# A gather-and-scatter graph layer: two tiles in 48 fetched row by row on two queues, three kinds of copies moved to VectorE, and first halves of 104 columns

## The chip, the cores and the metric

The kernel runs on one core of one Trainium2 chip. A core has five engines that run their own instruction streams and wait for each other through semaphores: TensorE (PE, with its weight loads as PEld), VectorE (DVE), ScalarE (ACT), GpSimd (POOL) and SyncE (SP). ACT, POOL and SP can start DMAs. The metric is the device time of one execution in microseconds (us); the median of three runs before the change is 2020.3 us (2017.76 to 2020.92).

## The reference

One graph layer with pre-normalisation: layer norm and ReLU over 12,500 nodes of 256 features, then, for 212,500 edges sorted by destination, the sum over a node's edges of its source's row times the weight of the edge's type (8 types), a self product, a bias, and the input added. Every node has one self-loop, the last of its edges, and about 16 others.

```python
h = jnp.maximum(_layernorm(x, axis=-1), 0.0)
hx = jnp.einsum('ni,rio->rno', h, weight)
agg = segment_sum(hx[edge_type, src], dst, num_segments=12500)
out = x + agg * 0.5**0.5 + h_bias + (h @ loop_weight) * 0.5**0.5
```

## The kernel before

**Units, tiles, windows.** The kernel sums rows of h by destination and type first and multiplies by the weights afterwards. Edges are cut into 802 units. The first 128 units have 256 edges each; the next ones 267 edges, of which each node's last edge (its self-loop) is taken out and the 256 others are kept, packed to the front of the unit (`compacted`); the last unit has the 41 edges that are left. A unit is one or two tiles of 128 kept edges: first half and second half (1603 tiles, the last unit has one). A unit's destinations lie in a window of WIN = 22 nodes that starts at `base`, the unit's first destination held between two bounds that lines 1082 to 1088 compute; the last of these holds both bounds between 0 and N - WIN.

For each tile a one-hot matrix of 128 edges by 22 x 8 columns (node in the window and type) is made on DVE (line 785), from a column number for each edge that `columns` computes (lines 481 to 585). `REACH` says from which node of the window each half's columns begin and how many nodes they span; an edge whose column lies outside is masked (line 558 for units of 267, lines 503 and 507 for the first block) and its column becomes 0. PE multiplies the gathered rows by the one-hot (line 818, fp32) into a PSUM bank, DVE adds the bank to a ring of sums `acc` (line 832), and when a group of 128 nodes is complete, 18 matmuls (line 1009) and two additions (1021, 1022) give its output.

**Gathers.** Rows come from x, for the first tiles, later from h32, the normalised table in HBM. POOL gathers a tile with one indirect DMA (line 755), 58 tiles ahead, into one of 60 slots. Of every 48 tiles one is not gathered by POOL: SP reads 16 byte offsets at a time from the tile `single` (line 762) and starts one DMA of 1 KB for each row (line 767), four list entries for each tile step (`fetch`), from 8 tile steps after the gather would have been issued. SP's queue also carries the loads of x, h, edges and weights and the stores of the output.

**Self-loops.** `find_types` finds the type of each node's self-loop and `begin` writes the node's own row into the ring through a PSUM tile `pt` (line 881). Three kinds of copies there run on ACT: `self_t` from `pt` (line 864, 98), a diagonal (line 934, 88) and the types (line 945, 22).

**The verdict.** Each unit counts the edges that its masks and its self-loops cover. `verdict` (lines 613 to 631) adds the counts, compares them with E and sets `flag`; every engine reads the flag, and at line 1243 the program branches: where the flag is set, `general_path` (lines 120 to 216) computes all of the output once more, with one node tile or 128 edges a round.

```python
# 622   def differs(): nc.vector.tensor_scalar(flag, pt[0:1, 0:1], float(E), None, op0=ALU.not_equal)
# 1087  nc.vector.tensor_scalar(
# 1088      whole, f, 0.0, float(max(0, N - WIN)), op0=ALU.max, op1=ALU.min)
# 210   for body, total in ((nodes, N), (edges, E)):
# 212       with tc.For_i(0, total // P * P, P) as i:
# 213           body(i, P)
# 1243  with tc.If(state["general"]):
# 1244      general_path(tc, x, src, dst, etype, bias, out, h32, w, wl, ident)
```

`nodes` (lines 146 to 171) loads 128 rows of h32 and x, transposes h, multiplies it by the self weight and by the eight type weights, one PSUM tile after another, and stores 1 MB of products into `hx` and the self part into `gacc`. `edges` (lines 173 to 208) loads source, destination and type of 128 edges and the destinations as a row (lines 179, 183), makes two columns of row numbers on DVE, gathers 128 rows of `hx` (line 199), adds those of equal destination with one matmul (line 203), copies the result out of PSUM and adds it to `gacc` with an indirect DMA (line 206). All pools of general_path have one buffer. At the end `gacc` is copied to the output (line 216).

Of the kernel before, what the change touches and what calls it, by code (L numbers as in the profile page):

```python
# [13 lines left out]
AF = mybir.ActivationFunctionType  # L14
ALU = mybir.AluOpType
# [3 lines left out]
SYNC_DEP = mybir.DependencyInfo(mybir.DependencyClass.Sync, mybir.DependencyReason.DATA)  # L19
DVE = mybir.EngineType.DVE  # L20
SP = mybir.EngineType.SP

P = 128
EPS = 1e-5
# [3 lines left out]
XG = 4  # L28
# [4 lines left out]


WIN = 22
REACH = ((0, 22), (4, 18))

GROUP = 128

# [5 lines left out]
AHEAD = 58  # L45

SINGLE = 48
FETCH = 4
SOURCES = 16
HOLD = 8  # L50


# [2 lines left out]
PAIR = 2  # L55
# [164 lines left out]
def kernel(  # L220
# [11 lines left out]
    nc = tc.nc  # L232
    N, D = x.shape
    E = src.shape[0]
    R = weight.shape[0]
# [5 lines left out]
    NT = plan.NT  # L241
# [33 lines left out]

    def place_of(t):
        u, i = divmod(t, PAIR)
        return u // P, i, u % P


    with ExitStack() as main:
# [29 lines left out]
        msg, oh, offsets, kind = {}, {}, {}, {}  # L311
        firsts, stops, loops, marked, typed, gidx, col = {}, {}, {}, {}, {}, {}, {}
        added, zeroed = {}, {}
        single, fetches = {}, []
        state = {"h32": None}


# [39 lines left out]
        def kept_sources(b, got):  # L357

            def keep():
                single[b] = idx.tile([P, P], I32, name="single")  # L360
                nc.vector.tensor_single_scalar(
                    single[b], got["sf"][:, P:U], float(D * 4), op=ALU.mult)

            return [keep]

# [115 lines left out]
        def columns(b, got):  # L481
# [22 lines left out]
                        got["there"][:, h], got["col"][:, h], float(o), None, op0=ALU.is_ge)  # L504

            def plain_to():
                nc.vector.scalar_tensor_tensor(
                    got["there"][:, :U], got["col"][:, :U], float(WIN), got["there"][:, :U],
                    op0=ALU.is_lt, op1=ALU.mult)

            def plain_typed():
                nc.vector.scalar_tensor_tensor(
# [226 lines left out]
        def gather(t):  # L739
            if t % PAIR == 0:  # L740
                both = msgs.tile([P, PAIR, D], F32, name="msg")
                for i in range(PAIR):
                    msg[t + i] = both[:, i, :]
            if t % QUAD:
                kind[t] = kind[t - 1]
            else:
                kind[t] = "h" if state["h32"] is not None and t >= state["h32"] + LATE else "x"
            table = {"h": h32, "x": x}[kind[t]]
            b, i, u = place_of(t)
            if b and i and kind[t] == "h" and t % SINGLE == SINGLE - 1 and t + AHEAD < NT:  # L750
                for r in range(0, P, SOURCES):
                    fetches.append((done["tile"] + HOLD, lambda r=r: load_sources(t, r)))
                return
            at = i * P + u
            nc.gpsimd.indirect_dma_start(  # L755
                out=msg[t], out_offset=None, in_=table[:, :],
                in_offset=bass.IndirectOffsetOnAxis(ap=gidx[b][:, at : at + 1], axis=0))

        def load_sources(t, r0):

            b, _, u = place_of(t)
            _, vals = nc.values_load_multi_w_load_instructions(  # L762
                single[b][u : u + 1, r0 : r0 + SOURCES], engines=[SP],
                min_val=0, max_val=(N - 1) * D * 4,
                skip_runtime_bounds_check_because="clamped to the table where they are computed")
            for i, v in reversed(list(enumerate(vals))):
                fetches.insert(0, (0, lambda i=i, v=v: nc.sync.dma_start(  # L767
                    msg[t][r0 + i : r0 + i + 1, :].bitcast(U8),
                    h32_bytes[:, bass.ds(v, D * 4)])))

        def fetch(n):
            for _ in range(n):
                if fetches and fetches[0][0] <= done["tile"]:
                    fetches.pop(0)[1]()

        def onehots(t):

            n = min(QUAD, NT - t)
            o = ohs.tile([P, QUAD // PAIR, PAIR, C], F32, tag="oh", name="oh")
            b, _, u = place_of(t)  # L780
            k = 0
            for v, i in ((n // PAIR, PAIR), (1, n % PAIR)):
                if v and i:
                    of = col[b].rearrange("p (i u) -> p u i", i=PAIR)[:, u + k : u + k + v, :i]
                    j = nc.vector.tensor_tensor(  # L785
                        o[:, k : k + v, :i, :],
                        iota_f.unsqueeze(1).unsqueeze(1).to_broadcast([P, v, i, C]),
                        of.unsqueeze(3).to_broadcast([P, v, i, C]), op=ALU.is_equal)
                    k += v
            for i in range(n):  # L790
                oh[t + i] = o[:, i // PAIR, i % PAIR, :]
                made[t + i] = j.ins.name

        def load_offsets(u0):
# [8 lines left out]
        def edge_sums(t):  # L803
            m, o = msg.pop(t), oh.pop(t)
            if t % PAIR == 0:
                bank = banks[t // PAIR % BANKS]
                sums["ps"] = bank[:, : KC * R * WIN].rearrange("p (c k) -> p c k", c=KC)
            ps = sums["ps"]
            i = t % PAIR
            from_, width = (a * R for a in REACH[i])  # L810
            end = t == NT - 1 or i == PAIR - 1
            free = added.get(t // PAIR - BANKS)
            if i == 0 and free is not None and latest["pe"] is not None:
                tc.add_manual_dep(latest["pe"], free.name, SYNC_DEP, reason="bank is free")
            if i == 0 and latest["pe"] is not None:
                tc.add_manual_dep(latest["pe"], made[t], SYNC_DEP, reason="one-hots are made")
            for c in range(KC):
                j = nc.tensor.matmul(  # L818
                    ps[:, c, from_ : from_ + width], m[:, c * P : (c + 1) * P], o[:, :width],
                    start=(i == 0 and c == 0), stop=(end and c == KC - 1))  # L820
            latest["pe"] = j.ins
            return ps
# [28 lines left out]
        def turn_nodes(g, pool, written=None):  # L851

            n = plan.ends[g] - plan.starts[g]
            pst = pt[:, : KC * P].rearrange("p (c d) -> p c d", c=KC)

            def turn():
                rows_ = got["h", g // XG][:, g % XG, :]
                for c in range(KC):
                    nc.tensor.transpose(  # L859
                        pst[:, c, :n], rows_[:n, c * P : (c + 1) * P], ident[:n, :n])  # L860

            def keep():
                got["self", g] = pool.tile([P, KC, GROUP], F32, name="self_t")
                i = nc.scalar.activation(got["self", g][:, :, :n], pst[:, :, :n], AF.Copy)  # L864
                if written:
                    tc.add_manual_dep(
                        i.ins, written[0].name, SYNC_DEP, reason="one reader at a time")

            return turn, keep, pst

        def begin(g):

            n = plan.ends[g] - plan.starts[g]
            q, k = divmod(g, XG)
            written = []
            turn, keep, pst = turn_nodes(g, selves, written)
            s0 = g % SLOTS * GROUP

            def own(r):
                of = typed[q][:, k * GROUP : k * GROUP + n].unsqueeze(1).to_broadcast([P, KC, n])  # L880
                i = nc.vector.scalar_tensor_tensor(  # L881
                    acc[:, :, r, s0 : s0 + n], of, float(r + 1), pst[:, :, :n],
                    op0=ALU.is_equal, op1=ALU.mult)
                if r == R - 1:
                    zeroed[g, "slot"] = i.ins
                    written.append(i.ins)
# [20 lines left out]
        def find_types(q):  # L907
# [11 lines left out]
            def kinds_of():  # L919
# [45 lines left out]
        def group_ahead(g):  # L965
# [11 lines left out]
            if q < plan.typed:  # L977
                def turned_nodes():
                    turn, keep, _ = turn_nodes(g, early)
                    shared(turn, [(1, keep)])  # L980

                work.append((0.4, turned_nodes))
            if k == XG - 2:
# [286 lines left out]
```

## Time and profile before

| what | value |
|---|---|
| median of 3 runs | 2020.3 us |
| the profiled execution, its time | 2023.05 us |
| its span, first to last instruction | 2021.3 us |
| mean granted clock of PE | 0.957 |
| DMA, mean over the span | 139 GB/s |
| matmuls with one-hots, line 818: 128x176 / 128x144 | 645.8 / 562.2 us busy |
| matmuls with weights, line 1009, on sums | 883.0 us busy |
| ACT copies of line 864 / 934 / 945 | 37.5 / 28.1 / 13.1 us busy |
| SP's row DMAs, line 767 | 3456 of 1 KB, 228 ns each at the queue |
| SP's register loads, line 762 | 216, median 1261 ns |

A profile row has a line of the program, an engine and an operation with a count, the busy time and the mean of one; after the bar stands how long the engine sat idle just before, and what ended that. "issue" is time in which an engine waited for nothing that the profile shows. The timeline gives start, duration, engine, line and count; the chain of waits goes back from the last instruction to what released it at each step. SPq, ACTq, POOLq and so on are the sequencers in front of the engines.

### The profile page before, as it was taken

Reading aid. Unit: us, or ns where it says so; the run is one execution under the profiler, and the core shown is the slowest. Engines: PE = TensorE matmul, PEld = TensorE weight load, DVE = VectorE, ACT = ScalarE, POOL = GpSimd, SP = SyncE. Lnnn points to the kernel's source line nnn. Section 1 sums busy time; section 2 is a strip of 40 time slices with the busy share of each in tenths; the row PEclk is TensorE's granted clock in tenths of the full one; section 3 lists DMA queues with packets and bytes.
Section 4 is the critical chain, followed back from the end, with each engine's and each line's share of the span. In section 5 each row is a group of like instructions: output and inputs, shape, how many; then the busy total and the mean of one; then the engine's idle time right before and its main releaser. Section 6 shows DMA issues by size and latency. Waiting matters only on the chain.

```text
span 2021.3 us, 36386 instructions
## 1 busy us (share of the span) xinstructions
PE 1796.2 (89%) x10411; PEld 1610.0 (80%) x10411; DVE 1317.4 (65%) x3281; ACT 218.4 (11%) x470; POOL 1500.7 (74%) x1602
## 2 busy tenths in 40 slices
PE   2468999997999898999899999998998898998998
PEld 2357999997888888988788788787787787787886
DVE  7869566687656578656577655577665568665642
ACT  7854110000000000000000000000000000000000
POOL 7766777777777777777777777777777777777773
PEclk8569999998999999999999999999999999999999
DMA  8973443444444444444444444444444444444442
GB/s 296 380 222 97 146 138 106 128 138 127 129 139 118 139 137 117 130 118 139 130 126 139 128 124 135 132 122 140 129 118 138 125 123 129 118 138 123 118 120 73
DMA packets 152577, 281.63 MB, mean 139 GB/s; under 512 B 31149, under 2 KB 101940, under 8 KB 152372
## 3 DMA queue, kind: packets, MB, share of 16 engines
q0 software_dynamic: 75648, 206.67, 35.1%
q1 hardware_dynamic: 76724, 72.61, 11.4%
q8 instruction: 82, 1.34, 0.3%
q14 instruction: 123, 1.01, 0.2%
HBM read 253.55 MB, written 25.60 MB: 138 GB/s over the span
## 4 chain that ended last, share of the span: by engine, by line
PE 38%; DMA 20%; SPq 17%; issue 12%; POOL 7%; DVE 5%; ACT 2%; DVEq 0%; POOLq 0%; ACTq 0%
PE ps L818 20%; PE po L1009 17%; DMA msg<-h,gidx 13%; SPq L767 13%; POOL msg L755 7%; SPq L762 4%; DMA hr<-h 2%; DMA h<-xt 1%; DVE e_stats L701 1%; DVE acc L832 1%; ACT xt L713 1%; DMA xr<-in_x_dram 1%; DMA w<-in_L_gnn_weight_dram 1%; DMA msg<-h 1%; DVE oh L785 1%
## 5 line engine op out<-in xcount | busy, mean ns | idle before, releaser
L755 POOL DMA_INDIRECT msg<-h,gidx x1480 | 1407.7, 951 | 464.2 <-issue 371.1
L818 PE MATMUL ps<-oh,msg 128*128 128x176 f32 (+1 forms) x6412 | 1169.6, 312 | 201.5 <-DMA msg<-h,gidx 78.5
L818 PEld LDWEIGHTS ps<-oh,msg 128*128 128x128 f32 x6412 | 1037.8, 196 | 355.3 <-DMA msg<-h,gidx 159.1
L1009 PE MATMUL po<-w,acc 128*128 128x256 f32 x3136 | 883.0, 383 | 1.8 <-DVE acc L832 1.8
L832 DVE TENSOR_TENSOR acc<-acc,ps 128x352 f32 x802 | 415.1, 518 | 503.4 <-PE ps L818 499.1
L1009 PEld LDWEIGHTS po<-w,acc 128*128 128x128 f32 x3136 | 537.6, 192 | 25.3 <-DVE acc L832 2.6
L785 DVE TENSOR_TENSOR oh<-fixed,cols 128x704 f32<-128x704 f32 x402 | 353.0, 879 | 0.0
L881 DVE SCALAR_TENSOR_TENSOR acc<-types,pt 128x256 f32<-128x256 bf16 (+1 forms) x688 | 249.0, 411 | 77.5 <-PE pt L859 71.5
L864 ACT ACTIVATE self_t<-pt 128x256 f32<-128x256 f32 x98 | 37.5, 383 | 1456.4 <-DVE acc L881 1352.5
L755 POOL DMA_INDIRECT msg<-in_x_dram,gidx x96 | 91.0, 948 | 31.1 <-issue 24.4
L1009 PE MATMUL po<-wl,self_t 128*128 128x256 f32 x392 | 105.2, 391 | 4.9 <-ACT self_t L864 2.5
L1009 PEld LDWEIGHTS po<-wl,self_t 128*128 128x128 f32 x392 | 69.1, 196 | 11.4 <-ACT self_t L864 2.9
L1021 DVE TENSOR_TENSOR xr<-xr,po 128x256 f32<-128x256 f32 x98 | 40.5, 413 | 17.5 <-PE po L1009 15.7
L713 ACT ACTIVATE xt<-xt,n_shift,n_rstd 128x256 f32<-128x256 f32 x98 | 50.9, 588 | 8.6 <-DVE n_shift L710 8.6
L713 ACT ACTIVATE msg<-msg,e_shift,e_rstd 128x256 f32<-128x256 f32 x96 | 49.6, 589 | 12.8 <-DVE e_shift L710 12.8
L1022 DVE TENSOR_TENSOR xr<-xr,po 128x256 f32<-128x256 f32 x98 | 41.2, 420 | 3.4
L934 ACT ACTIVATE diagonal<-ident,kinds 128x128 bf16<-128x128 f32 x88 | 28.1, 390 | 135.0 <-DVE kinds L931 130.1
L859 PE MATMUL pt<-ident,hr 128*128 128x128 f32 x196 | 37.9, 275 | 0.0
L370 DVE TENSOR_SCALAR moves<-fixed 128x267 int32<-128x267 int32 x84 | 36.0, 428 | 1.1
L701 DVE BATCH_NORM_STATS2 n_stats<-xt 128x6 f32<-128x256 f32 x98 | 34.4, 412 | 2.5 <-DMA xt<-in_x_dram 1.7
L371 DVE COPY_PREDICATED fixed<-moves,fixed 128x266 int32<-128x266 int32 (+6 forms) x84 | 33.7, 401 | 2.9
L701 DVE BATCH_NORM_STATS2 e_stats<-msg 128x6 f32<-128x256 f32 x96 | 33.5, 411 | 0.0
(201 smaller groups left out, 319.7 us busy)
## 6 DMA issues: line engine op xcount, KB each, us to landing
msg<-h SPq DMA_DIRECT2D x3456, 1.0 KB
msg<-h,gidx POOLq DMA_INDIRECT x1480
xt<-in_x_dram SPq DMA_DIRECT2D x24, 512.0 KB
h<-xt SPq DMA_DIRECT2D x24, 512.0 KB
xr<-in_x_dram SPq DMA_DIRECT2D x24, 512.0 KB
hr<-h SPq DMA_DIRECT2D x24, 512.0 KB
out_dram<-xr SPq DMA_DIRECT2D x24, 512.0 KB
w<-in_L_gnn_weight_dram SPq DMA_DIRECT2D x2, 1024.0 KB
```

Of the source, the lines that this page charges most:

```text
L701: nc.vector.bn_stats(stats[:n, j, :], rows_[j])
L713: nc.scalar.activation(rows_[j], rows_[j], AF.Relu, bias=shift[:n, j : j + 1], scale=rstd[:n, j : j + 1])
L755: nc.gpsimd.indirect_dma_start(out=msg[t], out_offset=None, in_=table[:, :], in_offset=bass.IndirectOffsetOnAxis(ap=gidx[b][:, at : at + 1 ...
L762: _, vals = nc.values_load_multi_w_load_instructions(single[b][u : u + 1, r0 : r0 + SOURCES], engines=[SP], min_val=0, max_val=(N - 1) * D ...
L767: fetches.insert(0, (0, lambda i=i, v=v: nc.sync.dma_start(msg[t][r0 + i : r0 + i + 1, :].bitcast(U8), h32_bytes[:, bass.ds(v, D * 4)])))
L785: j = nc.vector.tensor_tensor(o[:, k : k + v, :i, :], iota_f.unsqueeze(1).unsqueeze(1).to_broadcast([P, v, i, C]), of.unsqueeze(3).to_broa ...
L818: j = nc.tensor.matmul(ps[:, c, from_ : from_ + width], m[:, c * P : (c + 1) * P], o[:, :width], start=(i == 0 and c == 0), stop=(end and ...
L832: i = nc.vector.tensor_tensor(a, a, ps, op=ALU.add)
L881: i = nc.vector.scalar_tensor_tensor(acc[:, :, r, s0 : s0 + n], of, float(r + 1), pst[:, :, :n], op0=ALU.is_equal, op1=ALU.mult)
L1009: i = nc.tensor.matmul(got["out", g][:n], lhs, rhs, start=(r == R and c == 0), stop=(r == R - 1 and c == KC - 1))
L1021: nc.vector.tensor_add(rows_[:n, k, :], rows_[:n, k, :], outs[g % 2][:n, 1, :])
L1022: nc.vector.tensor_add(rows_[:n, k, :], rows_[:n, k, :], got["out", g][:n])
```

## The change

SP fetches tiles 47 of 48 as before and ACT's queue, in the same manner, tiles 23 of 48; both read 32 offsets at a time. The two halves change places: the tile with the kept edges 128 to 255 comes first, over all 22 nodes of the window, and the tile with the first 128 comes second, over nodes 0 to 12, so 13 x 8 = 104 columns. A last unit with one tile keeps its edges in the first half. The copies of lines 864, 934 and 945 go from ACT to DVE (the four diagonals of a group of four as one operation). Line numbers behind line 21 grow by one to three. general_path, the verdict and lines 1082 to 1088 stay as they are.

```diff
-REACH = ((0, 22), (4, 18))
+REACH = ((0, 13), (0, 22))
-SOURCES = 16
+SOURCES = 32
     def place_of(t):
         u, i = divmod(t, PAIR)
-        return u // P, i, u % P
+        half = 0 if PAIR * u + 1 == NT else PAIR - 1 - i
+        return u // P, half, u % P
-        single, fetches = {}, []
+        single, fetches = {}, {SP: [], ACT: []}
...
-                    single[b], got["sf"][:, P:U], float(D * 4), op=ALU.mult)
+                    single[b], got["sf"][:, :P], float(D * 4), op=ALU.mult)
...
             def plain_to():
-                nc.vector.scalar_tensor_tensor(
-                    got["there"][:, :U], got["col"][:, :U], float(WIN), got["there"][:, :U],
-                    op0=ALU.is_lt, op1=ALU.mult)
+                for h, o, n in halves:
+                    nc.vector.scalar_tensor_tensor(
+                        got["there"][:, h], got["col"][:, h], float(o + n), got["there"][:, h],
+                        op0=ALU.is_lt, op1=ALU.mult)
...
-            if b and i and kind[t] == "h" and t % SINGLE == SINGLE - 1 and t + AHEAD < NT:
-                for r in range(0, P, SOURCES):
-                    fetches.append((done["tile"] + HOLD, lambda r=r: load_sources(t, r)))
-                return
+            if b and t % PAIR and kind[t] == "h" and t + AHEAD < NT:
+                engine = {SINGLE - 1: SP, SINGLE // 2 - 1: ACT}.get(t % SINGLE)
+                if engine is not None:
+                    for r in range(0, P, SOURCES):
+                        fetches[engine].append(
+                            (done["tile"] + HOLD, lambda r=r: load_sources(t, r, engine)))
+                    return
...
-                single[b][u : u + 1, r0 : r0 + SOURCES], engines=[SP],
+                single[b][u : u + 1, r0 : r0 + SOURCES], engines=[engine],
...
+            queue = {SP: nc.sync, ACT: nc.scalar}[engine]
             for i, v in reversed(list(enumerate(vals))):
-                fetches.insert(0, (0, lambda i=i, v=v: nc.sync.dma_start(
+                fetches[engine].insert(0, (0, lambda i=i, v=v: queue.dma_start(
...
-            from_, width = (a * R for a in REACH[i])
+            width = R * (REACH[0][1] if i else WIN)
...
-                    ps[:, c, from_ : from_ + width], m[:, c * P : (c + 1) * P], o[:, :width],
+                    ps[:, c, :width], m[:, c * P : (c + 1) * P], o[:, :width],
...
-                i = nc.scalar.activation(got["self", g][:, :, :n], pst[:, :, :n], AF.Copy)
-                if written:
-                    tc.add_manual_dep(
-                        i.ins, written[0].name, SYNC_DEP, reason="one reader at a time")
+                nc.vector.tensor_copy(got["self", g][:, :, :n], pst[:, :, :n])
...
-                for g in range(XG):
-                    nc.scalar.activation(
-                        marked[q][:, g * GROUP : (g + 1) * GROUP], ident, AF.Copy,
-                        scale=kinds[:, g : g + 1])
+                nc.vector.tensor_tensor(
+                    marked[q].rearrange("p (g k) -> p g k", g=XG),
+                    ident.unsqueeze(1).to_broadcast([P, XG, GROUP]),
+                    kinds.unsqueeze(2).to_broadcast([P, XG, GROUP]), op=ALU.mult)
...
-                nc.scalar.activation(typed[q], pt, AF.Copy)
+                nc.vector.tensor_copy(typed[q], pt)
-            shared(spread, [(1, types_of)], lambda: q in marked, wait=2)
+            shared(spread, [(2, types_of)], lambda: q in marked, wait=2)
```

More of the change, by code (lines that the diff above doesn't have):

```diff
@@ L21 @@
 SP = mybir.EngineType.SP
+ACT = mybir.EngineType.Activation
 P = 128
@@ L757, in gather, with load_sources @@
                 in_offset=bass.IndirectOffsetOnAxis(ap=gidx[b][:, at : at + 1], axis=0))
-        def load_sources(t, r0):
+        def load_sources(t, r0, engine):
             b, _, u = place_of(t)
             _, vals = nc.values_load_multi_w_load_instructions(
-                single[b][u : u + 1, r0 : r0 + SOURCES], engines=[SP],
+                single[b][u : u + 1, r0 : r0 + SOURCES], engines=[engine],
                 min_val=0, max_val=(N - 1) * D * 4,
                 skip_runtime_bounds_check_because="clamped to the table where they are computed")
+            queue = {SP: nc.sync, ACT: nc.scalar}[engine]
             for i, v in reversed(list(enumerate(vals))):
-                fetches.insert(0, (0, lambda i=i, v=v: nc.sync.dma_start(
+                fetches[engine].insert(0, (0, lambda i=i, v=v: queue.dma_start(
                     msg[t][r0 + i : r0 + i + 1, :].bitcast(U8),
@@ L771, in fetch @@
         def fetch(n):
-            for _ in range(n):
-                if fetches and fetches[0][0] <= done["tile"]:
-                    fetches.pop(0)[1]()
+            for list_ in fetches.values():
+                for _ in range(n):
+                    if list_ and list_[0][0] <= done["tile"]:
+                        list_.pop(0)[1]()
         def onehots(t):
@@ L790, in onehots @@
             for i in range(n):
-                oh[t + i] = o[:, i // PAIR, i % PAIR, :]
+                oh[t + i] = o[:, i // PAIR, place_of(t + i)[1], :]
                 made[t + i] = j.ins.name
@@ L849, in clear, with turn_nodes @@
             zeroed[g, "slot"] = i.ins
-        def turn_nodes(g, pool, written=None):
+        def turn_nodes(g, pool):
             n = plan.ends[g] - plan.starts[g]
@@ L874, in begin @@
             q, k = divmod(g, XG)
-            written = []
-            turn, keep, pst = turn_nodes(g, selves, written)
+            turn, keep, pst = turn_nodes(g, selves)
             s0 = g % SLOTS * GROUP
@@ L885, in own @@
                     zeroed[g, "slot"] = i.ins
-                    written.append(i.ins)
             def write():
@@ L979, in turned_nodes @@
                     turn, keep, _ = turn_nodes(g, early)
-                    shared(turn, [(1, keep)])
+                    shared(turn, [(2, keep)])
                 work.append((0.4, turned_nodes))
```

## The prediction

> **What bounds the kernel now.** I read the page first (busy shares, slices, groups), then the timeline of POOL and SP, then the chain of waits, then the events of the two lines where the program branches and ends.
>
> ```profile
> PE 1796.2 (89%) x10411; PEld 1610.0 (80%) x10411; DVE 1317.4 (65%) x3281; ACT 218.4 (11%) x470; POOL 1500.7 (74%) x1602
> ...
> POOL 7766777777777777777777777777777777777773
> ...
> L755 POOL DMA_INDIRECT msg<-h,gidx x1480 | 1407.7, 951 | 464.2 <-issue 371.1
> ```
>
> PE has the largest share, but POOL's row is the flat one: 7 in nearly every slice, and most of the idle time before its gathers is issue, a wait for nobody. The timeline of POOL, and that of SP's queue, say what a 7 is:
>
> ```profile
> 1003.51 0.94 POOL L755 DMA_INDIRECT msg<-h,gidx  x1 [0.30 <-issue]
> 1004.76 0.95 POOL L755 DMA_INDIRECT msg<-h,gidx  x1 [0.31 <-issue]
> ...
> 1008.52 0.95 POOL L755 DMA_INDIRECT msg<-h,gidx  x1 [0.30 <-issue]
> ```
> ```profile
> 863.00 51.86 SPq L767 DMA_DIRECT2D msg<-h  x128
> ```
>
> One gather every 1.252 us ((1008.52 - 1003.51) / 4), back to back: POOL is full. 1576 gathers at 1.252 are 1973 us, from 4.75 to 1996.6 us; PE waits for what they bring (78.5 us at matmuls and 159.1 at weight loads, in the view of waits) and then has some 25 us of its own. SP fetches 27 tiles in POOL's place, 51.9 us each.
>
> The chain of waits gives the durations of DMAs (start, us, what), from issue to landing:
>
> ```profile
> 0.82 2.06 DMA nat_s<-in_src_dram
> ...
> 48.44 5.29 DMA h<-xt
> ...
> 405.00 6.01 DMA nat_t<-in_edge_type_dram
> ...
> 1778.62 5.86 DMA msg<-h,gidx
> ...
> 1979.16 2.73 DMA msg<-h,gidx
> ```
>
> And the lines of the branch on the verdict (L1243) and of the end of the program (L1266), the sequencers' own events (count, min/median/max ns, first and last start):
>
> ```profile
> L1243 SPq EVENT_SEMAPHORE  x8: 17/17/17, 2018.2 to 2019.6; - x8
> ...
> L1243 POOLq COMPARE_BRANCH  x1: 45/45/45, 1989.1 to 1989.1; - x1
> L1243 POOLq INC_SWDGE_SEM  x1: 2016/2016/2016, 1993.3 to 1993.3; - x1
> ```
> ```profile
> L1266 SPq EVENT_SEMAPHORE  x14: 17/28/28, 2019.7 to 2021.3; - x14
> ```
>
> Each engine compares once and goes to the end; no line of general_path is in the trace. Whether that stays so decides this case.
>
> **The change, part by part: the windows.** The first half of a unit (its first 128 kept edges) may now lie in columns 0 to 12 of its window alone. For a unit whose window starts at its first node that is ample. But L1088 holds every window's start at or below N - WIN = 12500 - 22 = 12478. The last unit has 212500 - 32768 - 673 x 267 = 41 edges, and in the drawn inputs they begin at node 12498, as every node has a self-loop and some 16 more. Its offset is 12498 - 12478 = 20. Its 39 edges that are not self-loops belong to columns 20 and 21, and all lie in the first half. Before, the first half reached 22 columns, and they counted. Now L558 admits column numbers up to 13 x 8 = 104, and theirs begin at 20 x 8 + 1 = 161: their mask is 0. So counts adds up to 212461, not E = 212500, differs at L623 gives 1, and the branch at L1243 goes into general_path, which computes everything again. (Of the unit before, the offset is small enough; I find no other miss.) The integers are far below 2^24, and in the run of before the same comparison came out equal.
>
> **The cost of general_path.** The trace has no row of it, so each step is bounded by its nearest rows. All its pools have one buffer, and each round of its loops ends with all engines waiting for each other and for every DMA: nothing overlaps from round to round, so a round is the sum of its chain.
>
> A round of edges (1660, and one of 20 edges):
> - SP issues four loads. The kernel's first three started at 0.82, 1.28 and 1.75, 0.46 apart, and the first landed after 2.06; the third, the types, lands at 0.1 + 2 x 0.46 + 2.06 = 3.1 us. Upper end 7.0, with the 6.01 of nat_t. I take 3.1: nothing else moves then.
> - DVE casts the types (0.14, as L394) and makes the row number (0.16, as L600): 0.3. The other nine DVE operations lie before it or under the gather.
> - The gather: 2.73 to 5.86; 2.8, for an idle chip.
> - PE, one product of 256 columns: weights 0.19 and the pair of passes 0.59, 0.8; at half clock 1.6 (the window 50 to 100 us shows 0.50 granted).
> - DVE's copy out of PSUM: 0.47 with its gap (L351, 0.42).
> - The scatter that adds: no row. At least a gather, 2.73; at most one under load, 5.86; it also reads what it adds to. I take 4.1, between.
> - The end of the round: SP's last events run from 2019.6 to 2021.3, 1.7 us for the waits and two meetings of all engines; POOL's semaphore instruction has one row of 2.0 that may itself be a wait. 1.7 to 4.0, and 2.9 taken.
>
> Sum 14.5 us (11.9 to about 20 with several upper ends at once): 1661 x 14.5 = 24,085 us.
>
> A round of nodes (98): load 2.6 (issue 0.49, then as nat_s), transposes 0.4, copy 0.4, own product 0.9, eight times two products (0.86), a copy (0.42) and gaps (0.1), as the one PSUM tile makes them alternate, 11.0; the store of 1 MB, 0.5 and twice the 5.29 of the 512 KB store, 10.6; end 2.9. 28.8 us, so 2820 us in all. 22 to 40 us a round (store half as long; PE at half clock): 2150 to 3900.
>
> At last 12.8 MB go from gacc to the output: between 380 GB/s (the page's best slice) and its mean of 139, 34 to 92 us; 65 taken, and 10 for the set-up.
>
> **The other parts**, which change the first 2 ms. SP's queue keeps its 27 tiles; ACT takes 27 more from POOL: 27 x 1.252 = 33.8 us less on the path that sets the end. What hides the rest: a row costs SP (51.86 - 8 x 1.3) / 128 = 0.324 us, a tile 41.5 plus four register loads of 32 (1.26, L762's row for 16, to 2.52), 47 to 52 us, within the 46 x 1.252 = 57.6 between two such tiles. ACT has no DMA row in the trace; SP's is the nearest, and above 57.6 / 128 - 0.06 = 0.39 us a row ACT would become the bound. In ACT's queue nothing stands behind these rows in that stage, since its 98 copies (383 ns), 88 diagonals (390) and 22 types (597) move to DVE: about 98 x 0.42 + 22 x 0.66 + 22 x 0.66 = 70 us on an engine busy 1317 of 2021, hidden while DVE waits for PE (499 us before L832); without that cover 70 us more. The first halves' matmuls shrink from 144 to 104 columns: the chain has 0.60 us for a tile of 176 and 0.49 for one of 144, so 0.35 for 104, or 0.49 if the weight loads bind: 0 to 112 us of PE time, worth nothing while PE waits for gathers. The mask of the first block is made in two operations instead of one, and the halves change places: nothing that anyone waits for.
>
> **Sum**, against the profiled execution's 2021.3 us span: 2021.3 - 33.8 = 1987.5; + 2820 + 24,085 + 65 + 10 = 28,968. Some 1.75 us lie outside the span (2023.05), and the median, 2020.3, is 2.75 below that; next to 27 ms neither counts. I forecast 29,000 us.
>
> **Rivals.**
> - *The verdict holds and general_path is not entered* (the other side). Place: the compare at L1243; it decides if the last unit's window does not start at 12478. Then the time is 1987.5, and the 27 ms vanish. For it: the trace shows the branch not taken. Against: the sum above is integer arithmetic on the inputs. 0.03.
> - *Not entered, and ACT's queue binds*: at 0.45 us a row a tile takes 65 us, and 27 of them 1760 from about 340 us on, some 2110. 0.01: it needs the first miss too.
> - *Each round fetches its instructions anew.* The page's instruction queues show 82 and 123 packets for a program that runs straight on; no row shows a jump back. If each round waits for one or two DMAs at 2.06 us, 1759 rounds add 3600 to 7200, and the time is about 34,000. 0.15. The Trainium skill (Runtime: NRT & Kernel Launch, section Instruction fetch mechanics) speaks for it: a taken branch to code outside the two pages that an engine holds must wait for a DMA of that page. No run here shows it yet.
> - *Rounds overlap*, so that the loads and the gather of the next run under the scatter: some 8 us a round (5.5 for gather and scatter, 2.9 for the end), 18,000 in all. Against: one buffer for each tile and the wait at each round's end. 0.08.
>
> **How the numbers follow.** The forecast, general_path at about 14.5 us a round, has 0.73. Low end 23,000: 1987 + 2150 + 19,765 (11.9 a round) are 23,900, with a little room. High end 38,000: 20 us a round and 40 for nodes give 39,000 with nearly all upper ends at once; it also holds the refetching rival. What is left out is the two rivals at 2 ms, the overlap and a little at the top, under 0.2. A difference of 0.2% is about what a measurement can tell. Faster takes the first rival, 0.03; same 0.01, in case gains and ACT's cost cancel; slower 0.96.
>
> **What would show it.** Right: rows for L149 to L216 (shifted by the new lines), 1660 scatters on POOL, a PE row near 0 after slice 3, and POOL's last gather of msg near 1963 us. Wrong: a span near 1990 without such rows; or a round far from 14.5 us, and then the step whose duration differs. The fetch on ACT is right if PE does not wait for msg rows longer than before and the first stage ends 30 to 36 us sooner.

## The result, and the profile after

The changed kernel takes 27,488.57 us (median of 4 runs, 27,459.43 to 27,540.62), the kernel before 2019.53 us in runs beside it: 13.61 times as long (95% interval 13.591 to 13.639). The profiled execution took 27,540.62 us, with a span of 27,538.9 us. 29,000 us were predicted, 23,000 to 38,000.

The page of the changed kernel (rows of engines; tenths of busy time in 40 slices; costliest groups with busy time, mean ns and the idle time before):

```profile
PE 5303.2 (19%) x17457; PEld 3390.3 (12%) x17457; DVE 6275.1 (23%) x24434; ACT 140.2 (1%) x262; POOL 5748.4 (21%) x4900
...
PE   7766555300000000000000000000000000000000
...
POOL 7652000111111111111111111111111111111111
PEclk8887555555555555555555555555555555555555
...
L200 POOL DMA_INDIRECT g_m<-hx,g_of x1661 | 1643.2, 989 | 14405.7 <-DVE g_of L197 11648.4
L207 POOL DMA_INDIRECT gacc<-g_ss,g_to x1661 | 2630.1, 1583 | 6414.7 <-DVE g_ss L206 6414.7
...
L761 POOL DMA_INDIRECT msg<-h,gidx x1453 | 1381.4, 951 | 822.2 <-issue 370.1
...
L826 PE MATMUL ps<-oh,msg 128*128 128x176 f32 (+1 forms) x6412 | 1107.2, 305 | 632.5 <-DMA msg<-h 552.9
```

From line 21 on, lines stand one to eight further down than before: 818 is now 826, 832 is 840, 1243 is 1246. Lines 200 and 207 are general_path's gather and scatter: 1661 of each, one a round. A slice is 688 us. The first stage fills three and a half, the rounds of nodes the next four, and in the last 32 no engine is busy for more than two tenths. The last two rows tell of something else, in the first stage: POOL sat idle 822 us before its gathers (464 before the change), and PE 553 us for rows of `msg`.

The events of the branch (line 1243 before, 1246 now: count, min/median/max ns, first and last start):

```profile
L1246 POOLq COMPARE_BRANCH  x2: 48/48/49, 2321.4 to 27492.4; - x2
...
L1246 SPq COMPARE_BRANCH  x2: 37/45/53, 2401.1 to 27496.3; - x2
```

Each engine branches twice now, once into general_path and once at its end. SP, the last, enters at 2401 us and is back at 27,496: the first stage ends at 2402 instead of 2021, and everything behind it takes 25,137 us, of which the copy of `gacc` to the output is the last 42. Nodes run from 2402 to 5147, 28.0 us for each of 98 rounds; edges from 5147 to 27,497, 13.45 us for each of 1661.

The timeline of one edge round (start, duration, engine, line):

```profile
15000.37 0.15 DVE L181 CAST g_sf<-g_s 128x1 f32<-128x1 int32 x1 [7.33 <-DMA g_s<-in_src_dram]
...
15002.00 0.99 POOL L200 DMA_INDIRECT g_m<-hx,g_of  x1 [7.09 <-DVE g_of L197]
...
15004.94 1.19 PE L204 MATMUL g_ps<-g_m,g_same 128*128 128x256 f32 x2 [12.36 <-DMA g_m<-hx,g_of]
15006.17 0.42 DVE L206 COPY g_ss<-g_ps 128x256 f32<-128x256 f32 x1 [1.78 <-PE g_ps L204]
15006.87 1.58 POOL L207 DMA_INDIRECT gacc<-g_ss,g_to  x1 [3.89 <-DVE g_ss L206]
15011.72 0.33 SPq L179 DMA_DIRECT2D g_s<-in_src_dram  x1
```

and a piece of the chain of waits in the last rounds:

```profile
27481.02 3.86 DMA gacc<-g_ss,g_to
```

Nothing overlaps from round to round. From the gather's issue to PE are 2.9 us, PE takes 1.2 at half clock, and from its end to the scatter's issue are 0.7. By the events of the scatter's semaphore, it lands 3.8 us after its issue in the median (3.65 in the round shown, at 15,010.5), and the next round's first load starts 1.2 us behind the landing (0.87 to 1.24 in 1660 rounds).

The first stage, in windows of 400 us (busy us and instructions of PE, PEld, DVE, ACT, POOL; granted clock; DMA share; GB/s). After, and then before:

```profile
800.00:1200.00 400.00, 302.70 (x1802) 281.07 (x1800) 224.35 (x516) 0.00 (x0) 246.38 (x260) 0.87 0.37 107
```
```profile
800.00:1200.00 400.00, 367.03 (x2161) 332.52 (x2160) 256.94 (x586) 17.45 (x46) 302.69 (x320) 0.97 0.44 129
```

POOL issues 260 DMAs where it issued 320: it is no longer full. The view of waits (us in all, times, longest) before:

```profile
PE ps L818 <- DMA msg<-h: 45.5, 11, 10.4
```

and after:

```profile
PE ps L826 <- DMA msg<-h: 552.9, 34, 26.0
```
```profile
SPq L774 <- DMA msg<-h: 425.2, 783, 10.0
```

PE waited 34 times, up to 26 us, for tiles that were fetched row by row (11 times, 45.5 us in all, before), and SP's queue 783 times for the landing of a row before it issued one. The timelines of SP's and of ACT's queue (consecutive DMAs of one line are one entry):

```profile
1299.87 58.23 SPq L774 DMA_DIRECT2D msg<-h  x116
1358.20 0.41 SPq L1030 DMA_DIRECT2D out_dram<-xr  x1
1358.67 0.50 SPq L962 DMA_DIRECT2D hr<-h  x1
1364.32 13.78 SPq L774 DMA_DIRECT2D msg<-h  x32
```
```profile
1300.05 79.98 ACTq L774 DMA_DIRECT2D msg<-h  x151
```

Before, SP issued the 128 rows of a tile in 51.9 us (54.4 in the median of its tiles); now 116 in 58.2, and ACT 151 in 80. A tile's rows take 53 to 76 us, in the median 68 on SP and 64 on ACT. From one tile's first row to the next one's are 73.5 us on SP, (2256.2 - 344.0) / 26, against 57.65 before, (1842.5 - 343.7) / 26. The difference, 15.9 us, 26 times is 413 us; 2402 less the predicted 1987.5 is 414. That the two agree says only that the whole stage was stretched evenly. That the rows set its pace is seen from PE's waits for them, from POOL's free time, and from SP's queue, where 68 us of rows and 2.2 of a first register load leave little of the 73.5. The next question is why rows are slower on two queues.

**What a row waits for.** The trace has eight completion semaphores for the DMAs of SP and ACT together, handed out in turn in one list of all these DMAs. A DMA waits until the one that had its semaphore before, eight places up in the list, has landed. Before, all eight places were SP's; now the list mostly goes SP, ACT, SP, ACT (two thirds of the neighbours in it are rows of different queues), so each queue has about four rows in flight. I took each row's issue from the trace, and the landing of the DMA before it on its semaphore from the semaphore's events (400 to 2250 us; after, only three of the four semaphores that general_path does not use as well):

| | before | after |
|---|---|---|
| rows that wait for their semaphore, looked at | 3236 | 2392 |
| of them issued within 0.1 us after that landing | 9 | 1120 |
| issue to landing of a row, median | 1.67 us | 1.73 us |
| those 1120: time since the queue's row before, median | | 0.46 (SP), 0.43 us (ACT) |
| the other rows, median | 0.323 us | 0.323 (SP), 0.312 us (ACT) |

A row is hardly slower on its way (1.73 against 1.67 us). What changed is that 47% of the rows start the moment a semaphore comes free; 1.73 / 4 = 0.43 us is their spacing. The queues also halt each other. While one loads its next 32 offsets (2.2 to 2.3 us), the list goes on with rows of the other alone, and the first row behind the load has to wait for one of these: the pause becomes 3.3 to 6 us, and ends 1 to 2 us after the other queue has issued the row that had the semaphore. There are 67 such pauses, in 17 of SP's 27 tiles and 14 of ACT's. No run gives each queue semaphores of its own; that the sharing makes the loss rests on these times and on the experiments with the rows' places below.

### The profile page after: what moved, and what is told of

It reads as the page before. It is cut to its first block, busy times and chain, and to the rows that moved or that the text cites. A ratio compares the mean times of both kernels' runs of the same rounds, so it can differ in the third digit from the quotient of the medians.

```text
span 27538.9 us, 198278 instructions
## 1 busy us (share of the span) xinstructions
PE 5303.2 (19%) x17457; PEld 3390.3 (12%) x17457; DVE 6275.1 (23%) x24434; ACT 140.2 (1%) x262; POOL 5748.4 (21%) x4900
## 5 line engine op out<-in xcount | busy, mean ns | idle before, releaser
L204 PE MATMUL g_ps<-g_m,g_same 128*128 128x256 f32 x3322 | 1980.4, 700 | 20365.9 <-DMA g_m<-hx,g_of 20279.9
L200 POOL DMA_INDIRECT g_m<-hx,g_of x1661 | 1643.2, 989 | 14405.7 <-DVE g_of L197 11648.4
L207 POOL DMA_INDIRECT gacc<-g_ss,g_to x1661 | 2630.1, 1583 | 6414.7 <-DVE g_ss L206 6414.7
L204 PEld LDWEIGHTS g_ps<-g_m,g_same 128*128 128x128 f32 x3322 | 832.7, 311 | 21513.2 <-DVE g_to L195 21410.0
L167 PE MATMUL g_pr<-w,g_ht 128*128 128x256 f32 x3136 | 1327.6, 566 | 354.5 <-DVE g_hs L170 354.5
L206 DVE COPY g_ss<-g_ps 128x256 f32<-128x256 f32 x1661 | 705.7, 425 | 2827.3 <-PE g_ps L204 2827.3
L826 PE MATMUL ps<-oh,msg 128*128 128x176 f32 (+1 forms) x6412 | 1107.2, 305 | 632.5 <-DMA msg<-h 552.9
L167 PEld LDWEIGHTS g_pr<-w,g_ht 128*128 128x128 f32 x3136 | 791.4, 275 | 883.8 <-DVE g_hs L170 762.5
L185 DVE CAST g_same<-g_row 128x128 f32<-128x128 int32 x1661 | 478.8, 288 | 1777.1 <-DMA g_row<-in_dst_dram 1777.0
L188 DVE TENSOR_TENSOR g_earlier<-g_same,before 128x128 f32<-128x128 f32 x1661 | 486.0, 293 | 57.6
L186 DVE TENSOR_SCALAR g_same<-g_same,g_df 128x128 f32<-128x128 f32 x1661 | 475.2, 286 | 58.9
```

The source lines that it names most:

```text
L167: nc.tensor.matmul(pr[:n], ht[:, c, :n], w[:, c, r * D : (r + 1) * D], start=(c == 0), stop=(c == KC - 1))
L185: nc.vector.tensor_copy(same[:n, :n], row[:n, :n])
L186: nc.vector.tensor_scalar(same[:n, :n], same[:n, :n], c["d"][:n], None, op0=ALU.is_equal)
L188: nc.vector.tensor_mul(earlier[:n, :n], same[:n, :n], before[:n, :n])
L200: nc.gpsimd.indirect_dma_start(out=m[:n], out_offset=None, in_=hx[:, :], in_offset=bass.IndirectOffsetOnAxis(ap=of[:n, 0:1], axis=0))
L204: nc.tensor.matmul(ps[:n], same[:n, :n], m[:n], start=True, stop=True)
```

## The experiments

The kernels ran in three groups on other chips (e1, e3 to e5; e2, e6 to e8; e9 to e12), where the kernel before itself takes 2568, 2590 and 2566 us; so only ratios to it within a group are compared. Why it is slower there stays open, but it works under another limit, as the first stage of e2 shows, which is that of the kernel before:

```profile
L755 POOL DMA_INDIRECT msg<-h,gidx x1480 | 1407.8, 951 | 926.2 <-issue 363.8
```

POOL idles 926 us before the same 1480 gathers, where it idled 464 on the first chip, so it is not full there even before the change; and PE waits 194.2 us for SP's row tiles (45.5 on the first chip). A tile that SP alone fetches takes 71 us in the median of e3, of a period of 73.7 (54.4 of 57.65 on the first chip). So expectations that count 1.252 us for each gather of POOL do not hold there, and SP's rows alone already cost something.

S is the theory that the eight shared semaphores make the loss, H that rows of two queues slow each other on their way to memory (for which 1.73 against 1.67 us leaves little), Q that a row simply costs ACT some 0.55 us, L that every tile of ACT costs its share.

**e1: the window's bound put back where it does not bind.** The last unit's window may start at its first node.

```diff
-                    whole, f, 0.0, float(max(0, N - WIN)), op0=ALU.max, op1=ALU.min)
+                    whole, f, 0.0, float(max(0, N - 1)), op0=ALU.max, op1=ALU.min)
```

> The changed kernel with one constant of L1091 changed: windows may start as late as node N - 1 instead of N - WIN. If the last unit's window alone set the flag, no row of general_path is left and the time is that of the first stage of the changed kernel, 2390 to 2410 us (its last product ends near 2402). If something else also misses edges, the time stays near 27,490.

2841.43 us, 1.1048 of before (1.0995 to 1.1102), no row of general_path. The expected time was for a chip where before takes 2020 us, a ratio of 1.18 to 1.19. So one bound sends the program into the 25 ms, as the prediction said (that it is the last unit alone, and 39 edges, follows from the inputs; no run shows the count), and the rest of the change costs 10% by itself (19% by the trace on the first chip, 2402 / 2021). PE waits 538.9 us for rows. All kernels below but e2 hold this edit too.

**e2: the kernel before, with general_path always entered.**

```diff
-                nc.vector.tensor_scalar(flag, pt[0:1, 0:1], float(E), None, op0=ALU.not_equal)
+                nc.vector.tensor_scalar(flag, pt[0:1, 0:1], float(E + 1), None, op0=ALU.not_equal)
```

> The kernel before with the count compared to E+1, so that general_path runs although the counts agree; nothing of the first stage is changed. If general_path is entered by the flag alone and its price does not hang on the rest of the change, the branch is taken where the kernel before ends (within 10 us of its span) and the rest costs what it cost after the change, 25,137 us: nodes 28.0 us x 98, edges 13.45 us x 1661. On a chip where before takes 2,020 us that is 27,160. The rival, that the length of the rounds or the first stage's 381 us more belong together (the long program slows the first stage), expects the branch near 2,400 us here too.

One run, 27,833.46 us. SP's branch is at 2588.0 us, where the kernel before ends on this chip (2589.51 us), and 25,244 us follow, 0.4% more than the 25,137. So, as far as one run on another chip tells, the first stage does not feel the long program, and general_path's price does not depend on the rest of the change.

**e3 and e4: only one of the two queues fetches**, SP in e3, ACT in e4; POOL takes back the other's 27 tiles.

```diff
-                engine = {SINGLE - 1: SP, SINGLE // 2 - 1: ACT}.get(t % SINGLE)
+                engine = {SINGLE - 1: SP}.get(t % SINGLE)                # e3
+                engine = {SINGLE // 2 - 1: ACT}.get(t % SINGLE)          # e4
```

> As e1_clamp, but ACT fetches no rows: its 27 tiles go back to POOL, all else of the change stays. If the second row queue is what made the first stage 380 us longer, whatever the way, POOL sets the pace again: 1576 gathers at 1.252, 2005 to 2022 us, and the wait of PE for rows falls from 553 to under 60 us. If the copies that went to DVE, the 104 columns or the register loads of 32 have a share, it stays above 2035.

> As e1_clamp, but SP fetches no rows: only ACT does, its 27 tiles at the same places. Theory S (rows of both queues take turns on the program's eight DMA semaphores, and each waits for the DMA that had its semaphore before) and theory H (rows of two queues slow each other on the way to memory) both expect ACT alone to be as fast as SP alone: 0.30 to 0.35 us from row to row, and 2005 to 2025 us. Theory Q (a row costs ACT some 0.55 us, whatever SP does) expects 0.55 a row, some 72 us a tile and 2370 to 2400 us.

e3: 2557.83 us, 0.9962 (0.9936 to 0.9988). The narrower first halves, the copies on DVE and the larger register loads cost nothing together; all of e1's loss comes with ACT's 27 tiles. PE's wait for rows falls from e1's 538.9 to 166.2 us, not under 60 as expected from the first chip. e4: 2696.81 us, 1.0498 (1.0453 to 1.0542). ACT issues rows 0.312 us apart in the median, so Q falls, and still loses 5%, where S and H both expected it to be as fast as SP. Its queue and SP's over the same 55 us:

```profile
1599.93 55.00 ACTq L774 DMA_DIRECT2D msg<-h  x59
```
```profile
1643.49 0.38 SPq L1030 DMA_DIRECT2D out_dram<-xr  x1
```

59 rows in 55 us: from 1620.7 to 1647.4 ACT issued none. The DMA before it on that semaphore is SP's store of a group's output, which waits for DVE's sum and was issued at 1643.5. This is so in all of e4's 21 pauses of over 10 us: 13 end after such a store, 7 after SP's load `hr<-h`, one after a load of edges. So even with one queue fetching, the shared list ties ACT's rows to what SP's queue waits for. When SP does both, its own order has the same stores between the rows, and does not lose by it.

**e5: eight list entries a step instead of four**, which I thought would set the two queues' rows apart in the list.

```diff
-FETCH = 4
+FETCH = 8
```

> As e1_clamp with FETCH = 8: each queue's 132 entries are put into 17 tile steps instead of 33, so that the 24 steps between SP's tile and ACT's keep them apart in the order of the program. Theory S: in that order each tile's first row waits for rows of the tile before on the other queue, so that the queues take turns, 128 x 0.32 and four register loads of 2.2, 50 us for each, 100 us for 48 tiles: about 2,950 us (2,800 to 3,050). Theory H: the order of the program does not matter, the queues overlap as they like, 2,350 to 2,450 us; if rows slow each other only where they overlap, less.

One run, 2836.25 us, as e1. Neither expectation holds, for the experiment rested on a wrong idea: by the semaphores of its trace, the rows of SP and ACT alternate in the list just as in e1. It tells nothing apart.

**e6, e7, e8: fewer tiles, and another phase.** A tile in 64, with ACT's two tiles before SP's; a tile in 80 and in 96 with ACT's half a period away, as in the change.

```diff
-SINGLE = 48
+SINGLE = 64                                                              # e6; 80 in e7, 96 in e8
-                engine = {SINGLE - 1: SP, SINGLE // 2 - 1: ACT}.get(t % SINGLE)
+                engine = {SINGLE - 1: SP, SINGLE - 3: ACT}.get(t % SINGLE)   # e6 alone
```

> The clamp put back, SINGLE 64 and ACT's tile two before SP's: 20 tiles to each queue, 13 gathers fewer on POOL than before (13 x 1.252 = 16.3 us). Theory S (eight completion semaphores shared by the two queues in the order of the list; a pair of tiles takes 74 to 76 us together): POOL needs 62 x 1.252 = 77.6 us for its part of a period, so the rows just keep up, POOL is the bound again, and the time is 0.985 to 1.01 of before; rows are still spaced 0.43 to 0.46 us where both queues are at work. Rival L (each tile that ACT fetches costs its share, 0.1086 / 27 = 0.40% of the time as between e1 and e3): 20 x 0.40% on top of 0.99 = 1.07.

> The clamp put back and SINGLE 80: 16 tiles to each queue, half a period apart, 5 gathers fewer on POOL than before (6.3 us). A period is 78 x 1.252 = 97.7 us, a tile takes 48 to 75 us. S: both queues keep up, time 0.99 to 1.005 of before, PE's waits for rows of msg near those of e3 (166 us) and far from e1's 539. L: 16 x 0.40% = 1.06.

> The clamp put back and SINGLE 96: 13 tiles to each queue, the fetches of the two follow each other and hardly overlap, one gather more on POOL than before. S: with one queue at work at a time the rows go at 0.31 to 0.33 us again, and what is left is what e4 showed, ACT's rows held behind a store or load of SP that is waiting itself (4.98% - (-0.38%) = 5.4% for 27 tiles, so at most 2.6% for 13): 0.995 to 1.02. L: 13 x 0.40% = 1.05.

e6: 2606.5 us, 1.0054 (1.003 to 1.0077). e7: 2702.58, 1.0425 (1.0394 to 1.0456). e8: 2681.41, 1.0353 (1.0322 to 1.0383). L, a price per tile of ACT, falls: its 20 tiles in e6 cost least, its 13 in e8 3.5%. But e7 and e8 miss what S expected too, and their traces say why. The first row of a tile waits for its slot, which PE must have released; in e7 that row sits in the list between rows of the other queue's running tile. In 15 of SP's 16 tiles there SP stops for 19 to 29 us in the middle, and goes on within 2 us of the row of ACT that had its semaphore, which is the first of ACT's tile or one of the 25 behind it. Eight of ACT's 16 are held in the same way behind SP's first rows. In e8 SP stops so in 13 of its 14 tiles, for 13 to 34 us. In e6, with both tiles starting nearly together, no pause within a tile is over 13 us. So S has a second part, a block, besides the cap of eight in flight.

**e9 to e12: the block and the cap apart.** In e9 the phase alone is changed against e1, in e11 alone against e7; e10 is e6 at 72; e12 is e3 again.

```diff
-                engine = {SINGLE - 1: SP, SINGLE // 2 - 1: ACT}.get(t % SINGLE)
+                engine = {SINGLE - 1: SP, SINGLE - 3: ACT}.get(t % SINGLE)   # e9, e10, e11
-SINGLE = 48
+SINGLE = 72                                                              # e10; 80 in e11
```

> e1 with one edit: ACT's tile stands two before SP's instead of half a period away; 27 tiles to each queue as in e1. After e6 to e8 theory S has two parts: a cap (eight DMAs of SP and ACT together in flight, so that a pair of tiles takes 74 to 90 us whatever their phase) and a block (the first row of a tile waits for its buffer, and rows of the other queue with its semaphore wait behind it, 18 to 34 us in e7 and e8). S with both parts expects the cap to decide at 48, where POOL needs 46 x 1.252 = 57.6 us for a period: 1.07 to 1.11 of before on a chip where before takes about 2,570 (e1 1.105), 1.15 to 1.19 where it takes 2,020. If the block alone made the loss, the time is 0.99 to 1.02.

> e6 with SINGLE 72: 18 tiles to each queue, 9 gathers fewer on POOL than before (11.3 us), a period of 70 x 1.252 = 87.6 us for a pair of tiles that takes 74 to 90 us. S: the cap no longer binds or hardly, the block is small since both tiles start together: 0.990 to 1.003 of before, PE's waits for rows of msg at or under e6's 139 us. L (a price per tile of ACT, already hurt by e6): 18 x 0.40% = 1.06.

> e7 with one edit: ACT's tile two before SP's instead of half a period away; 16 tiles to each queue in both, 5 gathers fewer on POOL than before. S with the block expects e7's 4.3% to go nearly whole: 0.990 to 1.005 of before, PE's waits for rows of msg from 298 us to under 150, and no gap over 12 us within a tile of either queue. If phase does not matter it stays at 1.04.

> e3 again, beside the versions with both queues: the clamp put back, SP fetches its 27 tiles, ACT none, the rest of the change (104 columns first, copies on VectorE, 32 indices at a time) as it is. 0.994 to 1.002 of before; if it stays below e10 and e11, the second queue brings nothing at any of the spacings tried.

| | ratio to before | 95% interval | PE's waits for rows |
|---|---|---|---|
| e9, next to each other, 48 | 1.1505 | 1.147 to 1.154 | 616.7 us |
| e10, next to each other, 72 | 0.9833 | 0.9805 to 0.986 | 68.1 us |
| e11, next to each other, 80 | 0.9767 | 0.9737 to 0.9797 | 75.3 us |
| e12, SP alone, 48 | 0.9949 | 0.9926 to 0.9973 | 196.8 us |

The same line of the waits in e7 and in e11, which differ in ACT's phase alone:

```profile
PE ps L826 <- DMA msg<-h: 297.8, 20, 28.4
```
```profile
PE ps L826 <- DMA msg<-h: 75.3, 14, 12.4
```

Moving 16 tiles by 38 places takes the time from 1.0425 to 0.9767 of before (the two were measured in different groups, each against its own kernel before): that is the block. Within e11's tiles no pause is over 9 us. At 48 the same move does not help, which fits the cap, but e9 came out at 1.15 where 1.07 to 1.11 were expected: in its later tiles ACT's first rows wait up to 35 us for their slot behind their register load, and in 11 tiles SP's rows 14 to 25 us behind them. So the block is back, what the cap costs by itself is not shown, and why e9 is worse than e1 stays open. e10 and e11 came out better than expected. POOL's gathers saved are 9 and 5, at most 11.3 and 6.3 us, 0.4 and 0.2%, and POOL is not the limit there (it idles 887 us before its gathers in e12). The rows are the likelier cause, since PE waits 122 us less for them in e11 than in e12 and the span is 45 us shorter. That the two queues fetch 32 tiles with less waiting than SP its 27 is measured; how much of the 45 us it explains is argued. A rival was not run: SP alone with one tile in 80. SP has 16 tiles in e11 and 27 in e12, and 27 nearly fill its queue on these chips, so SP's smaller share may help by itself, whatever ACT adds.

e11 beats both kernels there: 2509.79 us (2495.59 to 2514.95) against 2565.5 (2557.33 to 2575.32) before and 2554.11 for e12. It was not run on a chip where before takes 2020 us; on that one PE waited only 45.5 us for rows before the change, so less is to be won.

## Why the prediction was right, and which step failed

**The verdict.** Right: the 20 columns' offset of the last unit, the masks, the branch. e1 removes that one bound and general_path with it; e2 adds general_path alone and gets the same 25 ms. The rivals in which it is not entered fall.

**The price of general_path**, 25,137 us against 26,980 predicted (2820 + 24,085 + 65 + 10). Step by step: nodes 28.0 us a round (28.8); edges 13.45 (14.5). In the edge round the loads and casts, from the first load's issue to the gather's, come to 3.6 us (3.1 and 0.3 predicted), the gather 2.9 (2.8), PE 1.2 (0.8; half clock was its upper end), the copy with its gaps 0.7 (0.47), the scatter 3.8 (4.1). The mis-sized term is the end of the round: 2.9 us were taken from the events at the program's end, and 1.2 was measured, below the range of 1.7 to 4.0. That alone is 1.7 x 1661, some 2,820 us; PE, the copy, the loads and the gather gave some of it back. The final copy took 42 us (34 to 92).

**Instructions fetched anew in each round.** Falls. The page counts the packets of the instruction queues, and the events of the loop's line say how often it went round:

```profile
q8 instruction: 83, 1.36, 0.0%
q14 instruction: 176, 1.44, 0.0%
```
```profile
L1269 SPq BRANCH_PREFETCH_HINT  x1757: 31/31/60, 2401.9 to 27472.3; - x196
```

Before, the same queues had 82 and 123 packets: 54 more for 1757 rounds, and the 1.2 us at the end of a round leave no room for a DMA of 2 us. The Trainium skill (Runtime: NRT & Kernel Launch, section Instruction fetch mechanics) lets a taken branch out of the engine's two pages wait for a fetch; these loops show no such wait. That does not speak against the rule: a round is short, some 92 recorded instructions on all engines together ((198,278 - 36,386) / 1759), so the jump may stay inside those pages, and each round has a prefetch hint of 31 ns in front of the jump.

**Overlapping rounds.** Falls: in the timeline each round's first load follows the scatter's landing.

**The first stage: the step that failed.** The prediction has POOL's 27 gathers less as 33.8 us less on the path, and took SP's 0.324 us for ACT's row, "the nearest", with 0.39 as the point from which ACT would bind. Each half of that was right alone: POOL did issue 27 fewer, and ACT's own row is 0.312 us (e4). What failed is that the two queues were priced as independent. With both at work a tile's rows take 68 us on SP and 64 on ACT, three register loads of 2.2 to 2.3 us among them; that is some 0.48 and 0.45 us a row, over that point, since rows wait for semaphores that the other queue holds. Instead of 1987.5 the stage ended at 2402, POOL's last gather started at 2327.7 instead of near 1963, and PE's waits for rows grew from 45.5 to 552.9 us, the sign that the prediction named for a wrong price of ACT's fetch. The rival with ACT binding came near the size, with 0.45 us a row and 65 us a tile, but by a price of ACT's own and not by sharing; its 2110 us were too few, as the period was 73.5 us, and its 0.01 was for a kernel without general_path. In 29,000 us the error of 414 is small and hides behind the shorter general_path, 1843 the other way; that the two cancel in part is luck.

The Trainium skill (DMA: Bandwidth & Descriptors, section Issuing engines are not separate DMA queues) says that starting DMAs from several engines saves no more than the sequencer's time to start them. The runs go further: in the first stage the second starting engine did not even save that, as e1 is 10% slower than before, by the traces through semaphores that both share.

**The rest of the change.** Next to nothing, as predicted: e3 and e12 are at 0.996 and 0.995. The terms behind it, from the groups by shape of the changed kernel:

```profile
L826 PE MATMUL ps<-oh,msg 128*128 128x104 f32 x3204 | 508.7, 283 | 601.4 <-DMA msg<-h 552.9 <-DVE acc L840 48.5
```
```profile
L872 DVE COPY self_t<-pt 128x256 f32<-128x256 f32 x98 | 40.9, 418 | 3.2 <-PE pt L867 3.2
L936 DVE TENSOR_TENSOR diagonal<-ident,kinds 128x512 bf16<-128x512 f32 x22 | 15.3, 695 | 0.8
L948 DVE CAST types<-pt 128x512 bf16<-128x512 f32 x22 | 15.2, 689 | 47.7 <-PE pt L944 47.6
```

Before:

```profile
L818 PE MATMUL ps<-oh,msg 128*128 128x144 f32 x3204 | 562.2, 298 | 131.7 <-DMA msg<-h 45.5 <-DVE acc L832 43.7 <-DMA msg<-h,gidx 41.1
```

The copies are 71 us on DVE (70). A matmul of 104 columns takes 283 ns where one of 144 took 298: 5% for 28% fewer columns. PE's busy time in them fell by 53.5 us, inside the predicted 0 to 112.

## What to carry to other kernels

A second DMA queue is not a second worker while both draw on one pool of completion semaphores: before pricing it, divide the time to landing by the DMAs that each queue can have in flight, and look at what the other queue waits for. Where both must be used, start their bursts together and leave a period longer than the burst, or the first transfer of one, waiting for its buffer, stops the other (e7 against e11, e9 against e10). And when a tightened range has a check with a slow path behind it, look first for the one input (here the last 41 edges) whose bound was set for the old range.

## What the runs showed of the hardware

- A row's DMA raises its semaphore twice: some 0.4 us after its issue, and when it lands, 1.67 us after the issue in the median (before). This agrees with the Trainium skill (DMA: Bandwidth & Descriptors, section Why a DMA increments its semaphore by 16 and not by 1): the sequencer writes the share of the unused DMA engines at once, and each engine used adds its own when its data is there.
- A meeting of all engines at the end of a loop's round, with the jump back, takes 1.2 us behind the last landing in the median (0.87 to 1.24).
- An indirect DMA that adds 128 rows of 1 KB in HBM took 1.58 us of POOL and 3.8 us to its landing, against 0.99 us of POOL and 2.9 us to the product that needs its rows for the plain gather.
- PE's granted clock followed its work: 0.97 between 800 and 1200 us before, 0.87 there after, when PE stood waiting more, and 0.50 in general_path.
